# A four-layer graph network on one core: row work of the last group, row buffers, and the end of the program

## The chip, the core and the metric

The kernel runs on one core of a Trainium2 chip. The metric is the device time of one execution in microseconds (us), as the median of several runs. A profile, taken in a separate execution, shows the engines: PE (TensorE) does matrix products into PSUM, DVE (VectorE) and ACT (ScalarE) work elementwise on SBUF and PSUM, POOL (GpSimd) works elementwise on SBUF, SP (SyncE) starts the transfers. PEld is the loading of weights into PE.

## The reference

There are 4096 nodes with 64 features (D = 64) and one adjacency matrix `adj` of 4096 x 4096 zeros and ones in fp32 (64 MB). Four layers follow one another, each as `x = layernorm(x + layer(x, adj))`. Cut to the core:

```python
# layer 0: mean over neighbours, linear, relu, rows to length 1
h = (adj @ X + X) / clip(deg + 1, 1)
out = relu(concat([X, h]) @ W + b);  out / max(norm(out), 1e-12)
# layers 1 and 3: hyperbolic attention (curvature c; c = 1 in layer 3)
adj_att = sigmoid(left[:, None] + right[None, :] + b_att) * adj
x_local = logmap(x[:, None, :], x[None, :, :])
support = einsum('ij,ijd->id', adj_att, x_local)
proj(expmap(x, support))
# layer 2: weight 0.5**(k - pos) for the neighbours in order of index
w = mask * where(pos > 0, 0.5 ** (k - pos), 0.0);  w @ (x @ weight) + bias
```

Since a layer needs every row of the one before, `adj` is read four times.

## The kernel before

`adj` is cut into 4 column stripes of WW = 1024 nodes. The rows of one stripe's nodes are a group; `GROUPS` is (3, 2, 1, 0), so group 0 is the last. A stripe goes over 32 blocks of 128 rows, two at a time (a pair, 1 MB by one transfer from SP's queue into one of six buffers), from block 31 down to 0. So a layer's first stripe needs group 3 at once and group 0 only for the last four pairs (`need((layer, 2 * g // WB))`).

In layers 1 and 3 `attend` does for each block: six matmuls into a PSUM tile z of 128x1024 (L1098 the edges, L1101 and L1104 the products of rows), on ACT the sigmoid of the attention into `sig` (L1113) and the square of z into `sq` (L1116), on DVE `t` = max(z, 0) x sig (L1119, z from PSUM). For each pair DVE then finishes `t` (L1121, 128x2048, `sq` and `t` from SBUF), and PE adds up `acc` from `t` and the row factors `xe` (L1076, eight matmuls), two pairs later. At the end of a stripe ACT copies `acc` to `sums` (L1127).

What happens between two stripes or layers on rows (row work) is written as generators. `move` carries a group's sums to its new rows (centre matmuls L1168, copies L1179, products L1184 and L1185, sums L1187 and L1189, then some 70 steps on 128x8 numbers with three inverse roots, three large steps L1265, L1266, L1269). For the last group it runs on DVE, for the others on GpSimd (`Small(on_pool)`). `end_0` is its counterpart for layer 0 and `end_2` for layer 2; both hand on to `norm_rows` (the layer norm, L896 to L911) and `prepare` (the row factors of the next attention layer, L917 to L1030), whose second half is itself put into a queue. An inverse root is a bit trick for the first value (L724 or L762) and three Newton rounds (L728 to L730 or L767 to L771).

The generators are run by `tick(n)`, called twice in a pair and once more at its end: each turn takes them on to their next `yield`, which gives the turns to wait. Such counts are how long one engine's work is expected to take before another's step is issued. `pool_done(small, large)` is the count for small and large steps on GpSimd; `soon`, `near` and `after` are others. A scheduler orders the instructions of each engine with these positions in view; in layers 0 and 2 PE and ACT keep the written order. An engine executes its instructions in that order, so a step that waits holds up all behind it.

In layer 0 (L1465) the pools m0_own and m0_sb hold `xw`, `sum_w`, `count_w` and the copies `top` and `low` of the accumulators (L1490, L1492). They are given back when the layer ends; the pools of layer 1, with `sig`, take the same space.

Of the kernel before, what the change touches and what calls it, by code (L numbers as in the profile page):

```python
# [19 lines left out]
P = 128  # L20
N = 4096
D = 64
# [29 lines left out]
ROOT2 = 2.0**0.5  # L52
LOG = (0.3333341, 0.1998662, 0.14984541)
# [7 lines left out]
def gnn_stack_kernel(  # L61
# [509 lines left out]
    def stream(fits):  # L571

        with ExitStack() as st:
# [74 lines left out]
            def soon():  # L648


                return 0 if place[0] in (0, 2) else 1
# [16 lines left out]

            spare, turn_of = [], [0]
# [50 lines left out]
            def rsqrt(a, name):  # L720
# [6 lines left out]
                for _ in range(3):  # L727
                    V.tensor_mul(t, r, r)  # L728
                    V.scalar_tensor_tensor(t, t, -0.5, a, ALU.mult, ALU.mult)
                    V.scalar_tensor_tensor(r, t, 1.5, r, ALU.add, ALU.mult)  # L730
                return r

            class Small:
# [19 lines left out]
                def wait(self, small, large=0):  # L753

                    return pool_done(small, large) if self.on_pool else soon()

                def rsqrt(self, a, name, small):

                    r, t = self.nums(name), self.nums("rs_t")
                    if self.on_pool:  # L760
                        yield self.wait(small)
# [4 lines left out]
                    for _ in range(3):  # L766
                        self.mul(t, r, r)  # L767
                        if self.on_pool:
                            self.mul(t, t, a)
                            self.ts(t, t, -0.5, 1.5, ALU.mult, ALU.add)  # L770
                            self.mul(r, t, r)  # L771
                        else:
                            self.stt(t, t, -0.5, a, ALU.mult, ALU.mult)
                            self.stt(r, t, 1.5, r, ALU.add, ALU.mult)
# [41 lines left out]
            def att_rows(w_att, name):  # L816

                t = row.tile([1, 2, 2, D], F32, name=name + "_row")
# [75 lines left out]
            def norm_rows(layer, s, v, x2_to):  # L894
# [12 lines left out]
                r = rsqrt(m, "n_r")  # L907
                yield soon()
                V.tensor_mul(x_of(layer)[:, blocks(s), :], v, over(r))
                V.tensor_mul(x2_to, r, r)  # L910
                V.tensor_mul(x2_to, x2_to, v2)  # L911
                yield soon()

            def prepare(layer, s, att, b_att, curve, least, good, small):
# [5 lines left out]
                V.tensor_scalar(cx2[:, at], x2[:, at], c, None, ALU.mult)  # L920
                V.tensor_scalar(bg, cx2[:, at], -1.0, 1.0, ALU.mult, ALU.add)
# [863 lines left out]
```

## Time and profile before

| what | us |
|---|---|
| median of 3 runs (1074.15 to 1074.6) | 1074.26 |
| the profiled execution's own time | 1069.06 |
| its span on the core | 1067.3 |
| PE busy | 982.1 (92%) |
| DVE busy | 920.2 (86%) |
| ACT busy | 754.3 (71%) |
| POOL busy | 270.8 (25%) |
| DVE L1119, 256 of mean 1.218 | 309.7 |
| DVE L1121, 128 of mean 2.306 | 295.2 |
| PE acc L1076, 1024 matmuls | 260.4 |
| DVE's waits for ACT's squares at L1119 | 14.9 |

Busy times of different engines overlap, so they don't add up to the span; the shares say how full an engine is over the whole. The "sums" copy of ACT (L1127) marks the end of each stripe: 287.05, 364.09, 442.33 and 517.38 in layer 1, and 809.77, 886.49, 962.96 and 1038.34 in layer 3. The layer-0 stripes end with L1490 at 53.64, 95.67, 139.26 and 181.06, the layer-2 accumulators are copied (L1685) at 610.20, 661.15 and 716.66.

### The profile page before, as it was taken

How to read it: one execution, taken by the hardware profiler on the slowest of the kernel's cores; microseconds unless marked ns; L12 is line 12 of the kernel's file. 1: busy time of each engine (PE TensorE's matmuls, PEld its weight loads, DVE VectorE, ACT ScalarE, POOL GpSimd, SP SyncE). 2: the span in 40 equal slices, each digit the busy share in tenths (PEclk: the TensorE clock that was granted, in tenths of full speed). 3: DMA queues.
4: the chain of work that ended last, by engine and by line, in shares of the span. 5: the costliest groups of instructions: out<-in, count | busy, mean ns of one | idle time of the engine just before them, and what ended most of it. 6: DMA issues, size and time to landing. Idle time of an engine off the chain costs nothing.

```text
span 1067.3 us, 13569 instructions
## 1 busy us (share of the span) xinstructions
PE 982.1 (92%) x4760; PEld 403.2 (38%) x4845; DVE 920.2 (86%) x1501; ACT 754.3 (71%) x877; POOL 270.8 (25%) x649
## 2 busy tenths in 40 slices
PE   5997998789999999999999999998899999999980
PEld 2454554333333333333333344443333333333320
DVE  8577887899999999999485489849999999999976
ACT  0013122779988899888677788898898888898850
POOL 0011212010044515435500010101102454444163
PEclk8899999989999999999999999999999999999985
DMA  9999999745656656757598999996465766666300
GB/s 364 356 426 364 383 395 375 277 175 197 233 204 230 215 206 202 249 184 249 205 363 332 371 346 316 324 321 222 138 236 190 250 216 208 241 228 234 131 1 24
DMA packets 38580, 271.62 MB, mean 254 GB/s; under 512 B 4710, under 2 KB 4710, under 8 KB 5734
## 3 DMA queue, kind: packets, MB, share of 16 engines
q1 hardware_dynamic: 37728, 270.03, 69.3%
q8 instruction: 40, 0.66, 0.2%
q10 hardware_dynamic: 774, 0.63, 0.2%
q14 instruction: 38, 0.31, 0.1%
HBM read 269.58 MB, written 1.05 MB: 254 GB/s over the span
## 4 chain that ended last, share of the span: by engine, by line
PE 66%; DVE 22%; ACT 5%; DMA 2%; POOL 2%; issue 2%; ACTq 0%; SPq 0%; POOLq 0%
PE acc L1076 17%; PE z L1641 11%; PE z L1101 8%; PE z L1098 7%; PE z L1104 7%; DVE t L1119 7%; DVE t L1121 6%; PE acc L1465 6%; PE z L1653 3%; DVE junk L844 2%; PE z L1607 2%; DMA edges<-in_adj_dram 2%; ACT sq L1648 1%; ACT sq L1116 1%; POOL sq L1435 1%
## 5 line engine op out<-in xcount | busy, mean ns | idle before, releaser
L1119 DVE SCALAR_TENSOR_TENSOR t<-z,sig 128x1024 f32<-128x1024 f32 x256 | 309.7, 1218 | 16.9 <-ACT sq L1116 14.9
L1121 DVE SCALAR_TENSOR_TENSOR t<-sq,t 128x2048 f32<-128x2048 f32 x128 | 295.2, 2306 | 0.2
L1116 ACT ACTIVATE sq<-z 128x1024 f32<-128x1024 f32 x256 | 254.3, 1021 | 56.5 <-PE z L1104 21.6
L1113 ACT ACTIVATE sig<-left_b,right 128x1024 f32<-128x1024 f32 x256 | 286.9, 1149 | 5.3 <-DVE t L1119 4.5
L1076 PE MATMUL acc<-t,xe 128*64 128x512 f32 x1024 | 260.4, 614 | 10.9 <-DVE t L1121 9.3
L1101 PE MATMUL z<-lo_hi,hi_lo 128*128 128x512 f16 x512 | 193.7, 378 | 3.8 <-issue 0.9
L1104 PE MATMUL z<-dst,src 74*128 74x512 f16 x512 | 194.7, 380 | 0.0
L1098 PE MATMUL z<-edges,two_i 128*128 128x512 bf16 x463 | 181.7, 392 | 5.4 <-DVE t L1119 5.4
L1648 ACT ACTIVATE sq<-z 128x512 bf16<-128x512 f32 (+1 forms) x192 | 137.6, 740 | 40.1 <-PE z L1641 39.5
L1076 PEld LDWEIGHTS acc<-t,xe 128*64 128x64 f32 x1024 | 64.3, 137 | 140.6 <-issue 106.5
L1098 PEld LDWEIGHTS <-two_i 128*128 128x128 bf16 x512 | 50.2, 98 | 120.7 <-issue 74.5
L1465 PE MATMUL acc<-edges,first 128*128 128x512 bf16 x241 | 77.9, 400 | 16.5 <-DMA edges<-in_adj_dram 15.9
L1641 PE MATMUL z<-edges,pass_by 128*128 128x512 bf16 x240 | 84.7, 388 | 7.3 <-ACT sq L1648 6.0
L844 DVE SCALAR_TENSOR_TENSOR t<-edges 128x2048 bf16<-128x2048 f32 x32 | 73.0, 2287 | 19.6 <-DMA edges<-in_adj_dram 19.2
L1641 PE MATMUL z<-edges,enter 128*128 128x512 bf16 x251 | 86.8, 387 | 0.5
L844 DVE SCALAR_TENSOR_TENSOR junk<-edges 128x2048 bf16<-128x2048 f32 x32 | 73.1, 2284 | 13.1 <-DMA edges<-in_adj_dram 13.1
L1465 PE MATMUL acc<-edges,third 128*65 128x512 bf16 x256 | 80.9, 397 | 0.8 <-issue 0.2
L1104 PEld LDWEIGHTS <-src 74*128 74x128 f16 x512 | 49.1, 96 | 72.0 <-issue 9.2
L1101 PEld LDWEIGHTS <-hi_lo 128*128 128x128 f16 x512 | 50.2, 98 | 60.6 <-issue 14.5
L901 POOL TENSOR_TENSOR sq<-z 128x512 f32<-128x512 f32 x8 | 10.2, 1278 | 156.1 <-DVE z L900 144.8
L1184 POOL TENSOR_TENSOR w_att<-x,u 128x512 f32<-128x512 f32 x6 | 12.7, 2121 | 140.9 <-ACT u L1179 140.9
L1607 PE MATMUL z<-sq,halves 128*128 128x512 bf16 x120 | 45.1, 377 | 0.7 <-ACT sq L1648 0.5
(399 smaller groups left out, 965.0 us busy)
## 6 DMA issues: line engine op xcount, KB each, us to landing
edges<-in_adj_dram SPq DMA_DIRECT2D x256, 1024.0 KB, 4.9
x<-in_x_dram SPq DMA_DIRECT2D x4, 256.0 KB
out_dram<-x ACTq DMA_DIRECT2D x2, 256.0 KB
out_dram<-x SPq DMA_DIRECT2D x2, 256.0 KB
w_sb<-in_L_gnn_W_dram ACTq DMA_DIRECT2D x1, 32.0 KB, 4.8
w_twice<-in_L_gnn_weight_dram ACTq DMA_DIRECT2D x2, 16.0 KB, 4.8
given<-in_L_gnn_b_dram ACTq DMA_DIRECT2D x1, 0.2 KB
given<-in_L_gnn_bias_dram ACTq DMA_DIRECT2D x1, 0.2 KB
```

What stands on the lines that cost most here:

```text
L844: V.scalar_tensor_tensor(junk, a, 0.0, a, ALU.not_equal, ALU.not_equal, accum_out=odd[:, n : n + 1])
L1076: it = nc.tensor.matmul(acc[h * D : (h + 1) * D, :], xe[:, j, :], t[:, k, h * W : (h + 1) * W], start=j == BLOCKS[0], stop=j == BLOCKS[-1],)
L1098: nc.tensor.matmul(half, two_i, edge[:, at : at + W], start=True, stop=False)
L1101: nc.tensor.matmul(half, hi_lo[:, of], lo_hi[:, to], start=False, stop=False)
L1104: last = nc.tensor.matmul(half, src[:, of], dst[:, to], start=False, stop=True)
L1113: nc.scalar.activation(sig, left_b, AF.Sigmoid, bias=right[:, j : j + 1])
L1116: nc.scalar.activation(sq[:, k], zp, AF.Square, bias=ROOT + OFF, scale=-1.0 / UNIT)
L1119: V.scalar_tensor_tensor(t[:, k], zp, 0.0, sig, ALU.max, ALU.mult)
L1121: V.scalar_tensor_tensor(t, sq, HIGH**2, t, ALU.add, ALU.mult)
L1465: nc.tensor.matmul(accs[h][:m], lhs[:, j, :], edge[:, at : at + W], start=j == BLOCKS[0], stop=j == BLOCKS[-1],)
L1641: nc.tensor.matmul(z[:, h : h + W], lhs, rhs[:, h : h + W], start=j == BLOCKS[0], stop=True, skip_group_check=True,)
L1648: weighed[0] = nc.scalar.activation(w, z[:, :n], AF.Exp, bias=-(OFF_EDGE + CUT) * LN2, scale=-LN2)
```

## The change

It has five parts.

- In the first stripes of layers 1 and 3 the last group's rows are still in preparation. Its large (128x512) steps and inverse roots move from DVE to GpSimd, all but the roots' first value and the sums along rows; so do small steps between them. `far` gives the wait counts.
- The inverse root has one round of higher order and one Newton round in place of three Newton rounds: seven steps on DVE instead of nine after the first value, ten on GpSimd instead of twelve.
- Row buffers: `xw` lies in `halves`, `sum_w` and `count_w` in `keep`, `top` and `low` and the attention rows in row tiles, and the pool m0_sb goes.
- The wait counts for GpSimd are shorter outside layer 2 (`Small.wait`), and two `soon` turns in `move` are left out for it.
- At the end of the program the last pair's `t` is two tiles, each finished by a 128x1024 step and added up by itself. The last `move` (`straight`) puts both parts' centre matmuls into two z tiles; the square, the product and the last product with q read PSUM directly, and ACT copies only the column of sums. Besides, the copy of layer 2's last accumulator is on DVE instead of ACT.

The diff, cut to its core and with the common indentation of eight places left out (the repeated signature of `add_up`, the call of `att_rows` and the dropped pool are not shown):

```diff
@@ -50,6 +50,7 @@
+THIRD = 0.375**0.5
@@ -666,6 +667,11 @@
+    def far(small, large=0):
+        beat = {1: 0.8, 3: 0.4}.get(place[0], 1.6)
+        return 1 + int((small * 0.29 + large * 1.04 + 2.3) / beat)
@@ -724,10 +730,13 @@
         )
-        for _ in range(3):
-            V.tensor_mul(t, r, r)
-            V.scalar_tensor_tensor(t, t, -0.5, a, ALU.mult, ALU.mult)
-            V.scalar_tensor_tensor(r, t, 1.5, r, ALU.add, ALU.mult)
+        V.tensor_mul(t, r, r)
+        V.scalar_tensor_tensor(t, t, THIRD, a, ALU.mult, ALU.mult)
+        V.scalar_tensor_tensor(t, t, -10.0 / 3.0 * THIRD, t, ALU.add, ALU.mult)
+        V.scalar_tensor_tensor(r, t, 5.0 * THIRD**2, r, ALU.add, ALU.mult)
+        V.tensor_mul(t, r, r)
+        V.scalar_tensor_tensor(t, t, -0.5, a, ALU.mult, ALU.mult)
+        V.scalar_tensor_tensor(r, t, 1.5, r, ALU.add, ALU.mult)
         return r
@@ -752,26 +761,40 @@
-            return pool_done(small, large) if self.on_pool else soon()
+            if not self.on_pool:
+                return soon()
+            if place[0] == 2:
+                return pool_done(small, large)
+            return 1 + int((small * 0.29 + large * 1.04 + 2.3) / 1.6)
...
-            if self.on_pool:
+            if self.on_pool and small:
...
-            for _ in range(3):
+            self.mul(t, r, r)
+            if self.on_pool:
+                s = self.nums("rs_s")
+                self.mul(t, t, a)
+                self.ts(s, t, 0.375, -1.25, ALU.mult, ALU.add)
+                self.mul(t, t, s)
+                self.ts(t, t, 1.875, None, ALU.add)
+                self.mul(r, t, r)
...
-                if self.on_pool:
-                    self.mul(t, t, a)
-                    self.ts(t, t, -0.5, 1.5, ALU.mult, ALU.add)
-                    self.mul(r, t, r)
-                else:
-                    self.stt(t, t, -0.5, a, ALU.mult, ALU.mult)
-                    self.stt(r, t, 1.5, r, ALU.add, ALU.mult)
+                self.mul(t, t, a)
+                self.ts(t, t, -0.5, 1.5, ALU.mult, ALU.add)
+                self.mul(r, t, r)
+            else:
+                self.stt(t, t, THIRD, a, ALU.mult, ALU.mult)
+                self.stt(t, t, -10.0 / 3.0 * THIRD, t, ALU.add, ALU.mult)
+                self.stt(r, t, 5.0 * THIRD**2, r, ALU.add, ALU.mult)
+                self.mul(t, r, r)
+                self.stt(t, t, -0.5, a, ALU.mult, ALU.mult)
+                self.stt(r, t, 1.5, r, ALU.add, ALU.mult)
@@ -813,9 +836,13 @@
-    def att_rows(w_att, name):
...
-        t = row.tile([1, 2, 2, D], F32, name=name + "_row")
+    att_space = grp("xw")[:1].rearrange("o k f -> o (k f)")
...
+    def att_rows(w_att, n):
...
+        t = att_space[:, n * 4 * D : (n + 1) * 4 * D].rearrange(
+            "o (u k d) -> o u k d", u=2, k=2
+        )
@@ -896,20 +923,29 @@
+        pooled = s == GROUPS[-1]
+        E = nc.gpsimd if pooled else V
...
-        V.tensor_sub(v, v, over(m))
+        E.tensor_sub(v, v, over(m))
...
-        yield soon()
-        yield soon()
+        if pooled:
+            yield far(0, 2)
+        else:
+            yield soon()
+            yield soon()
...
-        r = rsqrt(m, "n_r")
-        yield soon()
-        V.tensor_mul(x_of(layer)[:, blocks(s), :], v, over(r))
-        V.tensor_mul(x2_to, r, r)
-        V.tensor_mul(x2_to, x2_to, v2)
-        yield soon()
+        if pooled:
+            r = yield from Small(True, "").rsqrt(m, "n_r", 0)
+        else:
+            r = rsqrt(m, "n_r")
+            yield soon()
+        E.tensor_mul(x2_to, r, r)
+        E.tensor_mul(x2_to, x2_to, v2)
+        E.tensor_mul(x_of(layer)[:, blocks(s), :], v, over(r))
+        if not pooled:
+            yield soon()
@@ -917,15 +953,19 @@
-        V.tensor_scalar(cx2[:, at], x2[:, at], c, None, ALU.mult)
-        V.tensor_scalar(bg, cx2[:, at], -1.0, 1.0, ALU.mult, ALU.add)
+        pooled = s == GROUPS[-1]
+        E = nc.gpsimd if pooled else V
+        E.tensor_scalar(cx2[:, at], x2[:, at], c, None, ALU.mult)
+        E.tensor_scalar(bg, cx2[:, at], -1.0, 1.0, ALU.mult, ALU.add)
+        if pooled:
+            yield far(14, 1)
...
-        V.tensor_scalar(rbg, rbg, -0.13, 0.0, ALU.max, ALU.min)
+        E.tensor_scalar(rbg, rbg, -0.13, 0.0, ALU.max, ALU.min)
...
-        V.tensor_scalar(ym, rbg, sc, None, ALU.mult)
-        V.tensor_mul(y, xg, over(ym))
+        E.tensor_scalar(ym, rbg, sc, None, ALU.mult)
+        E.tensor_mul(y, xg, over(ym))
@@ -944,27 +984,32 @@
-            V.tensor_sub(ys[:, :, D : 2 * D], y, ys[:, :, :D])
+            E.tensor_sub(ys[:, :, D : 2 * D], y, ys[:, :, :D])
...
-            yield 1
-            V.tensor_add(w, xg, over(g))
-            yield 1
-            V.tensor_mul(xe[:, at, :], w, over(m))
+            if not pooled:
+                yield 1
+            E.tensor_add(w, xg, over(g))
+            if not pooled:
+                yield 1
+            E.tensor_mul(xe[:, at, :], w, over(m))
...
-            rt = rsqrt(q1, "rt")
-            V.tensor_mul(t, q1, rt)
-            V.tensor_scalar(t, t, TOP, None, ALU.min)
-            V.tensor_scalar(q1, q1, QTOP, None, ALU.min)
+            if pooled:
+                rt = yield from Small(True, "").rsqrt(q1, "rt", 0)
+            else:
+                rt = rsqrt(q1, "rt")
+            E.tensor_mul(t, q1, rt)
+            E.tensor_scalar(t, t, TOP, None, ALU.min)
+            E.tensor_scalar(q1, q1, QTOP, None, ALU.min)
...
-            yield 2 * near()
+            yield far(10, 1) if pooled else 2 * near()
@@ -1028,7 +1073,7 @@
-        later(second(), True, after(small))
+        later(second(), True, far(2, 1) if pooled else after(small))
         yield 1
@@ -1109,6 +1154,9 @@
                     t = sb.tile([P, 2, WW], F32, name="t", bufs=3)
+                    ts = [t, t]
+                    if g == 0 and then is None and layer == 3:
+                        ts[0] = sb.tile([P, 2, WW], F32, name="t", bufs=3)
                 sig = sb.tile([P, WW], F32, name="sig", bufs=3)
@@ -1116,10 +1164,17 @@
-                V.scalar_tensor_tensor(t[:, k], zp, 0.0, sig, ALU.max, ALU.mult)
+                V.scalar_tensor_tensor(ts[k][:, k], zp, 0.0, sig, ALU.max, ALU.mult)
...
-            V.scalar_tensor_tensor(t, sq, HIGH**2, t, ALU.add, ALU.mult)
-            lag.append((g, t))
+            if ts[0] is t:
+                V.scalar_tensor_tensor(t, sq, HIGH**2, t, ALU.add, ALU.mult)
+                lag.append((g, t, (1, 0)))
+            else:
+                for k in (1, 0):
+                    V.scalar_tensor_tensor(
+                        ts[k][:, k], sq[:, k], HIGH**2, ts[k][:, k], ALU.add, ALU.mult
+                    )
+                    lag.append((g, ts[k], (k,)))
@@ -1160,7 +1215,37 @@
-        for part in range(2):
+        straight = last and layer == 3
+        parts = []
+        if straight:
...
+            def part_of(rows, part):
+                of = slice(2 * part, 2 * part + 2)
+                return rows.rearrange("p (h k) f -> p k h f", h=2)[:, of]
...
+            for part in range(2):
+                t = z_tile()[:, : 4 * (D + 1)].rearrange(
+                    "p (i h f) -> p i h f", i=2, h=2
+                )
+                for i in range(2):
+                    cols = slice((2 * part + i) * P, (2 * part + i + 1) * P)
+                    nc.tensor.matmul(
+                        t[:, i], sums[:, cols], centre, start=True, stop=True
+                    )
+                parts.append(t)
+            yield near()
+            for part, t in enumerate(parts):
+                nc.scalar.activation(part_of(sq, part), t[:, :, :, :D], AF.Square)
+                V.tensor_mul(part_of(w, part), part_of(xg, part), t[:, :, :, :D])
+            for part, t in enumerate(parts):
+                nc.scalar.copy(
+                    sum_1.rearrange("p (h k) -> p k h", h=2)[
+                        :, 2 * part : 2 * part + 2
+                    ],
+                    t[:, :, :, D],
+                )
+            yield near()
+        for part in () if straight else range(2):
@@ -1181,14 +1266,16 @@
-        E.tensor_mul(w, xg, u)
-        nc.scalar.activation(sq, u, AF.Square)
-        yield G.wait(0, 1) if G.on_pool else near()
+        if not straight:
+            E.tensor_mul(w, xg, u)
+            nc.scalar.activation(sq, u, AF.Square)
+            yield G.wait(0, 1) if G.on_pool else near()
...
-        yield soon()
-        yield soon()
+        if not G.on_pool:
+            yield soon()
+            yield soon()
@@ -1263,7 +1350,11 @@
         E.tensor_mul(w, xg, over(p))
-        E.tensor_mul(u, u, over(q))
+        if straight:
+            for part, t in enumerate(parts):
+                V.tensor_mul(part_of(u, part), t[:, :, :, :D], part_of(over(q), part))
+        else:
+            E.tensor_mul(u, u, over(q))
         yield soon()
@@ -1362,9 +1452,9 @@
-        xw = own.tile([P, NB, D], F32, name="xw")
-        sum_w = own.tile([P, D + 1], F32, name="sum_w")
-        count_w = own.tile([D + 1, D + 1], F32, name="count_w")
+        xw = halves.bitcast(F32)
+        sum_w = keep.tile([P, D + 1], F32, name="sum_w")
+        count_w = keep.tile([D + 1, D + 1], F32, name="count_w")
@@ -1436,11 +1526,17 @@
-            n = rsqrt(n2, "n")
-            yield 1
-            V.tensor_mul(z, z, over(n))
-            V.tensor_add(z, z, x0[:, blocks(s), :])
-            yield 1
+            if s == GROUPS[-1]:
+                n = yield from Small(True, "").rsqrt(n2, "n", 0)
+                nc.gpsimd.tensor_mul(z, z, over(n))
+                nc.gpsimd.tensor_add(z, z, x0[:, blocks(s), :])
+                yield far(10, 2)
+            else:
+                n = rsqrt(n2, "n")
+                yield 1
+                V.tensor_mul(z, z, over(n))
+                V.tensor_add(z, z, x0[:, blocks(s), :])
+                yield 1
@@ -1486,9 +1582,15 @@
-                    top = sb.tile([P, W], F32, name="top")
+                    top = row.tile([P, W], F32, name="sums", bufs=2)
...
-                    low = sb.tile([D + 1, W], F32, name="low")
+                    low = (
+                        row.tile([P, WB, D + 1], F32, name="u_1").rearrange(
+                            "p k f -> p (k f)"
+                        )[: D + 1, :W]
+                        if h
+                        else grp("w_att").rearrange("p k f -> p (k f)")[: D + 1]
+                    )
@@ -1682,7 +1784,10 @@
                 for to, acc in zip(sums, of):
-                    nc.scalar.copy(to, acc)
+                    if s == GROUPS[-1]:
+                        V.tensor_copy(to, acc)
+                    else:
+                        nc.scalar.copy(to, acc)
                 later(end_2(s, sums))
```

More of the change, by code (lines that the diff above doesn't have):

```diff
@@ L1069, in attend, with add_up @@
                 lag = []
-                def add_up(g, t, behind=None):
-                    for k in (1, 0):
+                def add_up(g, t, ks, behind=None):
+                    for k in ks:
                         j = 2 * g + k
@@ L1355, in stream @@
                 own = lp.enter_context(tc.tile_pool(name="m0_own", bufs=1))
-                sb = lp.enter_context(tc.tile_pool(name="m0_sb", bufs=2))
                 ps = lp.enter_context(tc.tile_pool(name="m0_ps", bufs=6, space=PSUM))
@@ L1401, in stream @@
                 nc.scalar.dma_start(sum_w[:D, :D], w0[D:, :])
-                att_rows1, att_rows3 = att_rows(w_att1, "att1"), att_rows(w_att3, "att3")
+                att_rows1, att_rows3 = att_rows(w_att1, 0), att_rows(w_att3, 1)
                 def own_part(at, t):
```

## The prediction

> **What bounds the kernel now.** I read the page's busy shares and its chain first: PE is busy 92% of the 1067.3 us span and holds 66% of the chain, DVE 86% and 22%. Such shares mix four layers, so I cut the span with the windows view (columns: window, its length, busy PE, PEld, DVE, ACT, POOL with instruction counts, granted clock, DMA share, GB/s):
>
> ```profile
> 200.00:225.00 25.00, 22.29 (x94) 7.46 (x96) 25.00 (x41) 21.54 (x23) 1.04 (x1) 1.00 0.58 199
> 225.00:250.00 25.00, 21.80 (x104) 8.87 (x105) 21.29 (x53) 19.07 (x22) 4.69 (x7) 0.86 0.33 114
> 250.00:275.00 25.00, 24.86 (x111) 9.16 (x112) 24.07 (x23) 24.31 (x26) 0.00 (x0) 1.00 0.71 250
> ...
> 750.00:775.00 25.00, 21.58 (x113) 8.67 (x114) 22.96 (x59) 20.17 (x24) 4.67 (x7) 0.93 0.40 143
> ...
> 950.00:975.00 25.00, 24.86 (x107) 8.53 (x109) 24.37 (x20) 21.94 (x24) 11.21 (x36) 1.00 0.65 221
> ...
> 1025.00:1050.00 25.00, 12.63 (x42) 4.27 (x39) 16.75 (x33) 4.96 (x8) 16.60 (x55) 0.65 0.01 2
> 1050.00:1068.00 18.00, 0.00 (x0) 0.00 (x0) 10.72 (x64) 0.21 (x1) 0.30 (x1) 0.50 0.09 33
> ```
>
> Three regimes. In a settled stripe of layers 1 and 3 PE is full (24.86 of 25): a pair costs it 4.62 us, DVE 2 x 1.13 + 2.20 = 4.47. Nothing taken from DVE there shortens it. In the first stripe of those layers DVE is full and PE idles: DVE also prepares the last group's rows. From the starts of the `sums` copy, L1127 (287.05, 364.09, 442.33, 517.38; 809.77, 886.49, 962.96, 1038.34) a settled stripe takes 75 to 78 us; the first one takes 102 in layer 1 (first z matmul 185.02) and 95.7 in layer 3 (714.08). That is the room: at most some 25 and 19 us, much of it PE's own start. The third regime is the end, 1032 to 1067, a chain of small steps. Layers 0 and 2 are held by transfers (0.93 of the engines in 175 to 200) and by PE. Their edits I cost at nothing: shorter roots there lie beside these, and the layer-0 copies into rows that now alternate wait for reads of a stripe earlier, 42 us back (L1490 at 53.64, 95.67, 139.26). Were that cover gone, it would be a root's 1.9 us per stripe.
>
> One more thing the trace shows: GpSimd and DVE delay each other (timelines; columns start, length, engine, operation).
>
> ```profile
> 1015.09 2.28 DVE L1121 SCALAR_TENSOR_TENSOR t<-sq,t 128x2048 f32<-128x2048 f32 x1
> ...
> 1015.20 2.23 POOL L767 TENSOR_TENSOR rs_t<-r_t 128x8 f32<-128x8 f32 x1
> ```
>
> That GpSimd step usually takes 0.20. It lasts as long as the L1121 begun just before it. The other way round, at the end of the program:
>
> ```profile
> 1046.96 0.17 DVE L747 SCALAR_TENSOR_TENSOR r_t<-rs_t,r_t 128x8 f32<-128x8 f32 x1
> 1047.16 0.90 DVE L767 TENSOR_TENSOR rs_t<-r_t 128x8 f32<-128x8 f32 x1
> 1048.09 0.96 DVE L747 SCALAR_TENSOR_TENSOR rs_t<-rs_t,t 128x8 f32<-128x8 f32 x1
> ...
> 1049.29 1.03 DVE L767 TENSOR_TENSOR rs_t<-r_t 128x8 f32<-128x8 f32 x1
> ```
>
> ```profile
> 1046.97 1.06 POOL L1265 TENSOR_TENSOR w_att<-x,p 128x512 f32<-128x512 f32 x1
> 1047.99 1.04 POOL L1266 TENSOR_TENSOR u<-u,q 128x512 f32<-128x512 f32 x1
> 1049.11 1.19 POOL L1269 TENSOR_TENSOR x<-u,w_att 128x512 f32<-128x512 f32 x1
> ```
>
> Three DVE steps of 0.17 wait out the three large GpSimd steps.
>
> **Layer 1's first stripe: buffers, GpSimd, shorter roots.** Removed from DVE: eight 128x512 steps (L1441, L1442, L900, L909, L928, L947, L953, L955), 0.60 each between L1119s = 4.8; three roots of ten steps, of which only the seed stays, and some dozen small steps: at 0.075 to 0.2 each, some 4.1 net. Together 8.9. The start also moves. In before, ACT's first sigmoid waits until DVE has read the buffers that `sig` lies over:
>
> ```profile
> ACT L1113 <- DVE z L1429: 5.3, 1, 5.3
> ```
>
> and the first L1119 stands behind L1433, the reduction and a root of 1.9 us: it starts at 193.66. With the rows moved, `sig` waits for nothing and L1119 stands before L1433 in DVE's order: about 189.2. The first L1121 comes at 192.5 instead of 197.85, a lead of 5.3.
>
> Added: waits of DVE for GpSimd, and whatever DVE holds behind a waiting step stands too, L1119 and L1121 above all, so PSUM tiles stay full and PE stops. I replayed the new order by hand with the rule that one of the two waits out the other: the mean (waits for two 128x512 steps of 1.04 that collide with an L1121) 1.8; the variance sum 1.1; the reciprocal 2.6; L1121s behind GpSimd's y and xe steps 1.6 and 0.9: 8.0 in all. So DVE gains 5.3 + 8.9 - 8.0 = 6, between 5 and 8 as I vary the phase. PE can't use all of it: with its busy windows and its slower clock (0.86 in one) put end to end, without any wait for DVE, the copy at 287.05 could come at 272 at best, and spread over pairs I get a lead of 4.6. I take **-4.5**; bounds -11 (half of the stalls gone, near PE's end) and -1 (5.3 alone, with stalls a half above mine). The faster stripe asks for transfers sooner; their share of 0.33 to 0.71 here leaves room.
>
> Here a rule speaks against the change. The Trainium skill, "Perfetto Trace Analysis", section Optimizing Scalar/DVE Operations, says of moves between GpSimd and DVE that, since they share a port, they might not help; "SBUF — State Buffer", section Who interferes with whom, narrows it: a DVE instruction with at most one SBUF input doesn't contend. L1119 reads z from PSUM and only `sig` from SBUF; L1121 reads two from SBUF. By the first rule the 4.8 us of large steps come back in full (8 x 1.04 us of GpSimd blocking), leaving 5.3 + 4.1 - 8.0, so about -1.4. By the rows, which show a block only beside L1121 (half of DVE's time), it is the sum above. I follow the rows.
>
> **Layer 3's first stripe.** The start gains 1.0: the copy of layer 2's last accumulator (two L1685 rows, 716.66 to 717.71, in ACT's row, which is busy 23.54 of 25 there) goes to DVE, which idles there from 714.6 to 718.67. Six 128x512 steps: 3.6; roots and small steps 2.3; two DVE waits for GpSimd of before (0.93 and 2.04) go: 3.0. Against it waits of 1.0 (variance), 3.65 (reciprocal, behind a whole L1121 on GpSimd's side), 0.8 and 2.4 (the logarithm on ACT now wants GpSimd's root): 7.9. PE has a bound here of about 802 against 809.8. DVE's sum says -2, the stalls lie late in the stripe where no slack follows; I take **-1**, between +3 and -7.5.
>
> **Settled stripes.** GpSimd's part of `move` has shorter wait counts: of the four waits 5 to 4, 6 to 4, 5 to 4, 8 to 6 turns, and two turns dropped, eight in all at 4.62 / 3 = 1.54 us each: it ends some 12 us sooner. PE binds here, so this earns nothing by itself; if DVE reaches its next step before GpSimd is done, it stalls with L1119 behind it. The free GpSimd time between L1121s is about 3.4, 10.2, 3.4 and 5.7 us for needs of 2.6, 7.3, 2.7 and 4.9: all fit. **+0.3**, at most +3.
>
> **The end.** Five terms:
> - the last 128x2048 step becomes two of 1.1, so four of the last eight accumulations start earlier. They run at 0.46 each now (PE row at 1034.61: 3.68 for eight). By the row alone the last step gives about -1.0. "TensorE: Matmul & The Clock Gate", section Part 1, wants some 3.4 us of sustained work for the full rate, so closing PE's pause of 1.0 before them might give the full 0.23: -2.8. The pause only halves and the clock is 0.65 in this window: -1.2;
> - both centre matmul pairs go back to back (1.24 each, ACT copies between them at present), squares and products from PSUM: `d` ends at 1043.05 instead of 1044.78: -1.75;
> - the root at 1046.55 to 1050.73 takes 4.18; nine clean steps are 1.83, and GpSimd is done sooner, so its three blocks vanish: -2.35;
> - three roots on DVE have two steps less, 6 x 0.20: -1.2;
> - the last u times q from PSUM in two halves: +0.1.
>
> Sum **-6.4**, between -5 and -8. The output transfer behind it (1062.43 to 1067.3) stays.
>
> **Sum.** -4.5 - 1 + 0.3 - 6.4 = -11.6 on the profiled execution, 1069.06, so 1057.5. The median of the runs shown is 1074.26, 0.5% above it; the same step gives **1062.7**.
>
> **Rivals.**
> - *Only the end pays* (0.21). The windows speak for it: in 200 to 225 DVE is full, and every us taken from it may return as a wait for GpSimd. Against it: the 5.3 us start is no exchange between engines. First stripes 0: -6.1, 1068.2.
> - *Waits cost more than the steps* (0.10), the other side. Each time that GpSimd starts just after an L1121, as at 1015.20, it loses 2.2 us, and DVE's dependent step then stands in front of the next L1121. I have 15.9 us of such waits in both first stripes; doubled they take 16 more: -11.6 + 16 = +4.4, 1078.7. The turning point is 27.5 us in total.
> - *PE binds throughout* (0.12): the waits halve, 8 us come back: -19.6, 1054.7. For it: seeds and waits stand several slots apart. Against it: PE's own start and clock cap what it can use.
> - *The change doesn't do what it says* (0.02): against it, in the new order the steps do stand in GpSimd's row, and DVE has 125 instructions less, GpSimd 46 more. That leaves 1074.
> - Forecast case 0.55.
>
> **How the numbers follow.** The forecast case spans 1058 to 1067: layer 1 and layer 3 vary by some 3 each, the end by 1.5. A measurement here tells 0.2%, 2.1 us, from no change. Of the slow case most is above that (0.07); same takes the rest, the unchanged case and the upper tail of "only the end" (0.05); faster 0.88. Range 1055.5 to 1071.
>
> **What would show it.** First L1119 of layer 1 near 189 and no 5.3 wait on ACT; the `sums` copies of layer 1 4 to 5 us sooner, the first of layer 3 another 1; DVE waits for GpSimd below 16 us in the two stripes; at the end `d` 1.7 us sooner after the copy, the root in 1.4 us, last copy to end of span in 23.7 instead of 29.0. It is wrong if DVE's row shows GpSimd waits above 20 us in a first stripe, if the settled stripes grow beyond 78 us, or if the last GpSimd move still runs beside the root.

## The result, and the profile after

The changed kernel takes 1068.19 us in the median of 7 runs (1063.63 to 1070.72), the kernel before 1074.06 (7 runs, 1070.35 to 1074.6): ratio 0.9952, interval 0.993 to 0.9974. By this ratio that is 5.1 us (the two medians differ by 5.9), where 11.6 were forecast. A second series of 22 runs gave 0.9954 (0.9935 to 0.9973). The windows of the profiled execution of the changed kernel, same columns and stretches as before:

```profile
200.00:225.00 25.00, 18.81 (x81) 6.32 (x79) 19.65 (x21) 17.32 (x18) 17.71 (x26) 1.00 0.64 220
225.00:250.00 25.00, 20.86 (x106) 8.18 (x104) 19.20 (x37) 19.32 (x23) 11.54 (x24) 0.86 0.29 90
250.00:275.00 25.00, 24.78 (x113) 9.16 (x112) 23.94 (x17) 24.59 (x26) 0.00 (x0) 1.00 0.70 247
...
750.00:775.00 25.00, 23.59 (x125) 9.28 (x123) 21.32 (x33) 23.36 (x26) 5.79 (x9) 1.00 0.56 194
...
950.00:975.00 25.00, 25.00 (x111) 8.99 (x107) 22.84 (x16) 22.05 (x25) 11.82 (x12) 1.00 0.64 221
...
1025.00:1050.00 25.00, 14.14 (x58) 4.76 (x56) 20.99 (x57) 7.87 (x12) 9.45 (x16) 0.84 0.04 14
1050.00:1068.00 18.00, 0.00 (x0) 0.00 (x0) 6.95 (x38) 0.00 (x0) 0.00 (x0) 0.58 0.05 17
```

From 200 to 225 DVE went from 25.00 to 19.65 busy, GpSimd from 1.04 to 17.71. But PE, which the relief was meant for, went down too, from 22.29 to 18.81. DVE was relieved and nobody used it.

The fastest and the slowest execution of one kernel lie 4 to 13 us apart, so I compare stages, taken from the starts of the copies. "Layer 1 start" runs from the last layer-0 copy to the end of the first eight sums of products; "rest" from there to the first `sums` copy; "layer 3 first" from the copy of layer 2's last accumulator to the `sums` copy; "last + end" is the last stripe and what follows, to the end of the span. All in us, from one profile each:

| kernel | layer 1 start | rest | layer 3 first | last + end |
|---|---|---|---|---|
| before | 20.1 | 84.9 | 93.1 | 104.3 |
| changed | 15.0 | 88.8 | 96.6 | 97.4 |
| changed, again (after_again) | 15.0 | 88.4 | 96.7 | 95.8 |
| no_gp | 15.0 | 85.2 | 92.3 | 96.7 |
| no_gp1 | 19.2 | 86.8 | 96.7 | 95.9 |
| no_gp3 | 15.0 | 88.5 | 93.3 | 96.1 |
| before_rows | 15.0 | 89.1 | 94.3 | 104.4 |
| no_gp_old_roots | 15.0 | 92.3 | 92.8 | 96.1 |
| ys_first | 15.0 | 86.7 | 96.8 | 96.4 |
| long_waits | 15.0 | 86.6 | 99.2 | 97.2 |
| mixed | 19.2 | 86.6 | 93.5 | 96.6 |
| rb_late3 | 18.1 | 88.2 | 92.3 | 96.8 |
| before_end | 20.6 | 84.8 | 93.0 | 103.8 |
| no_gp_old_counts | 18.1 | 85.2 | 93.4 | 102.5 |

So the end brought 7 to 8.6 us, layer 1's first stripe 1.3 to 1.6, and layer 3's took back 3.5. (The copy that opens it, now on DVE, starts 1.7 us sooner after the copy of the accumulator before it, so the net loss around it is 1.8.) The settled stripes of layer 1 are each within some 0.5 us of before (0.2 in sum); in layer 3 the second and third together are 1.0 longer in the changed kernel's profile and 2.0 in its repeat, most of it in the third (76.5 before, 77.2 and 78.2).

Where it goes in layer 1: DVE's steps that wait for GpSimd (timeline; the wait in front of a step and who ended it stand at the end of the row), and the two PE rows behind them:

```profile
205.18 0.69 DVE L924 TENSOR_REDUCE n_m<-z 128x8 f32<-128x512 f32 x1 [2.14 <-POOL z L1532]
...
211.35 0.69 DVE L936 TENSOR_REDUCE n_v<-sq 128x8 f32<-128x512 f32 x1 [0.93 <-POOL sq L930]
...
223.47 0.20 DVE L962 RECIPROCAL rb<-b 128x8 f32<-128x8 f32 x1 [2.23 <-POOL b L959]
```

```profile
230.44 1.03 PE L1023 MATMUL aux<-ident,ys 128*128 128x128 f16 x8 [4.14 <-POOL ys L987]
231.40 3.68 PE L1121 MATMUL acc<-t,xe 128*64 128x512 f32 x8
```

These three DVE waits are about those of the forecast (1.8, 1.1, 2.6). The 4.14 us is not in it: PE's transposes of the last group's `ys` stand in its queue ahead of sums and z that were ready, and `ys` now comes from GpSimd. After this pause eight sums take 3.68 instead of 1.94, which I call half rate, and DVE in turn stands 4.02 us for ACT's next square. In layer 3 the same happens through DVE (DVE timeline, then PE's):

```profile
737.57 0.20 DVE L962 RECIPROCAL rb<-b 128x8 f32<-128x8 f32 x1 [3.70 <-POOL b L959]
737.69 2.24 DVE L1170 SCALAR_TENSOR_TENSOR t<-sq,t 128x2048 f32<-128x2048 f32 x1
```

```profile
739.98 3.68 PE L1121 MATMUL acc<-t,xe 128*64 128x512 f32 x8 [3.82 <-DVE t L1170]
```

A step of 0.20 us waits 3.70; L1170 behind it waits too; PE has nothing to sum for 3.82 and then runs at half rate for another 3.68. One handoff costs PE 3.82 + 1.74 = 5.6 us. In the kernel before, DVE's only wait for GpSimd of over 0.4 us in this stripe is one of 0.93, and PE's longest pause is 1.48.

### The profile page after: what moved, and what is told of

Its sections match the earlier page's. It is cut to its first block, busy times and chain, and to the rows that moved or that the text cites. A ratio compares the mean times of both kernels' runs of the same rounds, so it can differ in the third digit from the quotient of the medians.

```text
span 1063.3 us, 13594 instructions
## 1 busy us (share of the span) xinstructions
PE 985.4 (93%) x4845; PEld 400.7 (38%) x4845; DVE 901.2 (85%) x1383; ACT 753.4 (71%) x876; POOL 339.1 (32%) x695
## 4 chain that ended last, share of the span: by engine, by line
PE 66%; DVE 18%; POOL 5%; DMA 4%; ACT 4%; issue 2%; ACTq 0%; SPq 0%; POOLq 0%; DVEq 0%
PE acc L1121 18%; PE z L1743 11%; PE z L1143 8%; PE z L1149 8%; PE z L1146 7%; DVE t L1170 5%; DVE t L1167 5%; PE acc L1561 4%; DMA edges<-in_adj_dram 3%; PE z L1755 3%; DVE junk L871 2%; PE z L1709 2%; ACT sq L1750 1%; ACT sq L1164 1%; POOL sq L1525 1%
## 5 line engine op out<-in xcount | busy, mean ns | idle before, releaser
L1170 DVE SCALAR_TENSOR_TENSOR t<-sq,t 128x2048 f32<-128x2048 f32 x127 | 293.4, 2311 | 0.3
L1143 PE MATMUL z<-edges,two_i 128*128 128x512 bf16 x512 | 200.3, 391 | 6.2 <-DVE t L1167 6.2
L1561 PE MATMUL acc<-edges,first 128*128 128x512 bf16 x256 | 81.1, 398 | 18.1 <-DMA edges<-in_adj_dram 17.9
L1743 PE MATMUL z<-edges,enter 128*128 128x512 bf16 x256 | 88.2, 387 | 0.0
L1270 POOL TENSOR_TENSOR w_att<-x,u 128x512 f32<-128x512 f32 x6 | 18.2, 3028 | 169.9 <-ACT u L1264 169.9
L1709 PE MATMUL z<-sq,halves 128*128 128x512 bf16 x128 | 48.1, 377 | 0.6 <-ACT sq L1750 0.6
L1525 POOL TENSOR_TENSOR sq<-z 128x512 f32<-128x512 f32 x4 | 10.1, 2526 | 117.2 <-DVE z L1523 97.4
```

The lines of the kernel that those rows point to most:

```text
L1143: nc.tensor.matmul(half, two_i, edge[:, at : at + W], start=True, stop=False)
L1170: V.scalar_tensor_tensor(t, sq, HIGH**2, t, ALU.add, ALU.mult)
L1561: nc.tensor.matmul(accs[h][:m], lhs[:, j, :], edge[:, at : at + W], start=j == BLOCKS[0], stop=j == BLOCKS[-1],)
L1743: nc.tensor.matmul(z[:, h : h + W], lhs, rhs[:, h : h + W], start=j == BLOCKS[0], stop=True, skip_group_check=True,)
```

## Experiments: which part costs, which pays

All are made from the changed kernel unless said otherwise, and every row of the table above is one of their profiles.

**GpSimd's share taken back, in both layers or in one.**

```diff
-                pooled = s == GROUPS[-1]
+                pooled = False                           # no_gp
+                pooled = s == GROUPS[-1] and layer == 3  # no_gp1
+                pooled = s == GROUPS[-1] and layer == 1  # no_gp3
```

(and likewise for the root n of layer 0's end in no_gp and no_gp1.)

> The changed kernel once more, as the yardstick for the three beside it. Both theories: 0.993 to 0.998 of the kernel before; layer 1's first stripe (last layer-0 copy to first sums copy) 104 to 106 us against 105 before, layer 3's first stripe (copy of layer 2's last accumulator to sums copy) 96 to 97 against 93 before, last sums copy to end of span 23 to 24 against 29.

> The changed kernel with the last group's roots and large steps back on VectorE in both layers; row buffers, shorter roots, shorter counts and the new end are kept. Theory A (waits between VectorE and GpSimd stop TensorE, and its slow clock after a pause adds to it): layer 1's first stripe 100 to 102, layer 3's 92 to 93, so 5 to 7 us below the changed kernel, ratio to before 0.987 to 0.990. Theory B (the moved steps do pay, and the missing gain went elsewhere, such as transfers): 4 us or more above the changed kernel, ratio to before 0.998 or more. Theory C (TensorE and transfers set the first stripes anyway): within 1 us of the changed kernel.

> The steps back on VectorE in layer 1 alone. Theory A: layer 1's first stripe 100 to 102 as without any moved step, layer 3's 96 to 97 as in the changed kernel; 2.5 to 4 us below the changed kernel. Theory B: layer 1's first stripe 107 or more. Theory C: both stripes as in the changed kernel within 1 us.

> The steps back on VectorE in layer 3 alone. Theory A: layer 3's first stripe 92 to 93.5, layer 1's as in the changed kernel; 3 to 4.5 us below the changed kernel. Theory B: layer 3's first stripe above 97. Theory C: both stripes as in the changed kernel within 1 us.

Measured ratios to before: no_gp 0.9892 (0.9858 to 0.9926), no_gp1 0.9916 (0.9884 to 0.9949), no_gp3 0.9911 (0.9878 to 0.9944), beside 0.9954 for the changed kernel. Theory A holds, B and C fall: with both starts undisturbed, the steps moved to GpSimd cost 3.2 to 3.6 us in layer 1's rest (no_gp against the changed kernel), and 3.4 to 4.4 in layer 3. Without them the change is worth 1.1%, the size of the forecast. The repeat of the changed kernel missed one expectation: its first stripe took 103.4, not 104 to 106.

no_gp1's whole first stripe (105.97) missed its 100 to 102, and its rest (86.8) is 1.6 above no_gp's, though its program for layer 1 is no_gp's. The windows of no_gp and of no_gp1, in this order, show what befell the start:

```profile
185.00:195.00 10.00, 9.82 (x70) 5.65 (x70) 6.62 (x9) 8.59 (x10) 1.04 (x1) 1.00 1.01 425
```

```profile
185.00:195.00 10.00, 9.17 (x51) 6.88 (x50) 1.90 (x6) 7.11 (x9) 0.00 (x0) 0.70 1.01 420
```

PE's granted clock was 0.70 there in this execution, and its start took 19.2 instead of 15.0. (Layer 0 ends 3.5 us later in no_gp1, but no_gp is at 1.00 throughout 180 to 205.) This befell four of the profiles (18.1 to 19.2 in the table), so start and rest are kept apart. Whether the slow start also explains the 1.6 of the rest stays open: no_gp_old_counts has such a start too, and a rest of 85.2.

**Only the row buffers, on the kernel before.** The edit: `xw`, `sum_w`, `count_w`, `top`, `low` and the attention rows moved as in the change, nothing else.

> The kernel before with only the row buffers moved. Theory A: the whole lead at the start of layer 1 is this part: ACT's 5.3 us wait goes, the first sum of products ends 15 us after the last layer-0 copy as in the changed kernel (20.1 before), and it lasts: layer 1's first stripe 99.5 to 101, ratio 0.994 to 0.997. Rival: VectorE is full behind it and the lead is lost by the end of the stripe: 103.5 to 105, ratio 0.999 or more. Everything from layer 1's second stripe on as before within 0.5 us a stripe.

Ratio 0.9988 (0.9969 to 1.0008): no difference that can be told. The lead is there (15.0 instead of 20.1) and is gone at the end (89.1 instead of 84.9): the rival was right. DVE's row in before_rows shows where:

```profile
264.45 2.36 DVE L1123 SCALAR_TENSOR_TENSOR t<-z,sig 128x1024 f32<-128x1024 f32 x2 [4.29 <-ACT sig L1117]
```

This is the thirteenth pair. Its `sig` needs the last group's `right`, which is finished 76.7 us after the last layer-0 copy, as late as ever (74.5 before). The pairs came earlier and waited for the rows. The expectation of everything else within 0.5 us a stripe missed: the second stripe is 1.3 shorter, layer 3's first 1.2 longer, the last stripe 1.8 shorter and what follows it 1.8 longer. So an edit can move other stages by 1 to 2 us. What a stage varies without any edit, the two profiles of the changed kernel show: 0.4 us in the rest, 0.1 in layer 3's first stripe, 1.6 in the last one and the end.

**The shorter roots taken back**, from no_gp: three rounds again in DVE's `rsqrt`.

> The kernel no_gp (no step of the last group on GpSimd) with VectorE's inverse roots of three rounds again. Theory D2 (the pairs that need the last group wait for its preparation, and a root costs this chain a slot between two large steps for each of its steps; the moved rows only pay if the chain is shorter too): layer 1's first stripe 103 to 105 as in before_rows (104.1; 100.2 in no_gp), with a wait of 3 to 5 us of VectorE for ACT's sig ahead of the thirteenth pair; layer 3's 93.5 to 95. Theory E (shorter roots only save their own VectorE time, some 1.5 us): 100.5 to 101.7 and 92.3 to 93.3, no such wait. Both: last sums copy to end of span 1.2 us longer than no_gp's 23.1.

Ratio 0.9953 (0.9933 to 0.9974). Layer 1's stripe is 107.3, its rest 7.1 us longer than no_gp's, more than either theory said, and the wait is there:

```profile
266.57 3.49 DVE L1164 SCALAR_TENSOR_TENSOR t<-z,sig 128x1024 f32<-128x1024 f32 x3 [5.89 <-ACT sig L1158]
```

D2 holds in layer 1, E falls. Most of a root's dependent steps stand between two large steps of DVE, as no_gp's row shows:

```profile
219.74 0.16 DVE L733 TENSOR_TENSOR rs_t<-n_r 128x8 f32<-128x8 f32 x1
219.82 1.22 DVE L1167 SCALAR_TENSOR_TENSOR t<-z,sig 128x1024 f32<-128x1024 f32 x1
220.95 0.16 DVE L734 SCALAR_TENSOR_TENSOR rs_t<-rs_t,n_m 128x8 f32<-128x8 f32 x1
```

I call such a place a slot: two steps less are up to two slots less. With shorter roots in no_gp, `right` is finished at 72.7 instead of 77.1, and pair thirteen no longer waits. These 4.4 us are not the whole 7.1: behind the missed date PE pauses too and then runs at half rate for some 6 us (z matmuls of 0.63 instead of 0.38, PE's row in no_gp_old_roots), worth about 3 us by an estimate from these rows.

```profile
267.85 0.59 PE L1140 MATMUL z<-edges,two_i 128*128 128x512 bf16 x1 [3.01 <-DVE t L1164]
268.23 0.63 PE L1143 MATMUL z<-lo_hi,hi_lo 128*128 128x512 f16 x1
```

Layer 3 (92.8, forecast 93.5 to 95 by D2) lies with E: no deadline was missed there. The end missed both: at 23.0 after the copy it did not lengthen, since this edit leaves alone the second root function, which the end uses.

**ys first on GpSimd.**

```diff
-                    E.tensor_sub(ys[:, :, D : 2 * D], y, ys[:, :, :D])   # behind copies and xw
+                    ys_low = E.tensor_sub(ys[:, :, D : 2 * D], y, ys[:, :, :D])
+                    for it in its: in_order(it.ins, ys_low.ins)          # copies, xw
```

> The changed kernel with one thing moved: for the last group GpSimd subtracts ys (which TensorE's transposes wait for) ahead of the small copies and of xw, instead of behind them. Theory A1 (TensorE standing 4.1 us for GpSimd's ys, and half clock after it, is the larger part of what layer 1 loses): the wait falls below 2 us and layer 1's first stripe to 100.3 to 101.7, from 103.4 to 103.8. Theory A2 (the waits of VectorE for GpSimd decide, TensorE's pause only takes time that VectorE could not have used): layer 1's first stripe within 0.8 us of the changed kernel. Both: layer 3's first stripe stays at 96 to 97, since TensorE didn't wait for ys there.

The rest falls from 88.4 to 88.8 to 86.7, the stripe to 101.6: A1's upper edge. But the wait is still 2.59, because `ys` itself meets an L1170 and lasts 2.54 instead of 1.1 (GpSimd's row, then PE's):

```profile
223.46 2.54 POOL L972 TENSOR_TENSOR ys<-y,ys 128x512 f16<-128x512 f32 x1 [0.73 <-ACT ys L971]
```

```profile
226.06 1.03 PE L1026 MATMUL aux<-ident,ys 128*128 128x128 f16 x8 [2.59 <-POOL ys L972]
227.03 3.68 PE L1124 MATMUL acc<-t,xe 128*64 128x512 f32 x8
```

So this order takes back about 2 us of the 3.2 to 3.6, by one profile. What is left isn't divided: the shorter pause with its half rate and DVE's waits, unchanged here (2.14, 0.93, 2.23), both stand. Ratio 0.9946 (0.9924 to 0.9967), not told from the changed kernel by time alone.

**All of the preparation's wait counts doubled**, `beat = {1: 0.4, 3: 0.2}.get(place[0], 0.8)`.

> The changed kernel with the wait counts of the last group's preparation doubled, so that VectorE meets the sums, the reciprocal and the next steps one to three pairs later. Theory A2 (VectorE comes too early and stands with the pairs behind it): its waits for GpSimd (n_m 2.1, n_v 0.9, rb 2.2 in layer 1; n_v 1.2, rb 3.7 in layer 3) fall below 1 us in each stripe, layer 3's first stripe to 93 to 94.5 from 96.6, layer 1's to 100 to 102. Theory D (the longer chain on GpSimd itself is the cost, and only changes the place of the wait): both stripes as long as in the changed kernel within 0.8 us, or longer, with the wait at the transposes or at the pairs that need group 0.

Ratio 0.9953 (0.9932 to 0.9974). Half of each theory: DVE's waits for GpSimd are gone in layer 1 (the twelfth L1170 starts 65.6 us after the last layer-0 copy, 79.0 in the changed kernel), but the rows come late (`right` at 73.6 instead of 66.0) and the thirteenth starts only at 80.1. The stripe, 101.5, lies in A2's range all the same. In layer 3 the stripe grows to 99.2, as D said. There PE stands at the transposes, by now behind ACT:

```profile
769.10 1.01 PE L1023 MATMUL aux<-ident,ys 128*128 128x128 f16 x8 [4.95 <-ACT hi_lo L1027]
770.04 3.67 PE L1121 MATMUL acc<-t,xe 128*64 128x512 f32 x8
```

**One wait alone, one pair later, in layer 3.**

```diff
-                    yield far(14, 1)
+                    yield far(14, 1, 1.6 if layer == 3 else 1.0)   # last: factor on the count
```

> The changed kernel with one count longer: in layer 3 VectorE meets the last group's reciprocal one pair later (two L1119 steps and one L1121 step more in front of it). If VectorE's 3.7 us wait there, TensorE's pause of 3.8 us and the half clock after it are what layer 3 loses: the wait falls below 0.5 us, the 3.68 us for eight sums returns to 1.94, and layer 3's first stripe is 92.5 to 94.5 (96.65 in the changed kernel, 93.1 before). If the later end of the preparation takes it back: 96 or more, with waits at the transposes. Layer 1 as in the changed kernel; ratio to before 0.990 to 0.994.

DVE's order differs by one pair in front of one reciprocal. DVE's and PE's rows answer to the two of the changed kernel above:

```profile
742.33 0.20 DVE L962 RECIPROCAL rb<-b 128x8 f32<-128x8 f32 x1 [1.09 <-POOL b L959]
```

```profile
744.75 1.94 PE L1121 MATMUL acc<-t,xe 128*64 128x512 f32 x8 [1.18 <-DVE t L1170]
```

The wait is 1.09 (not below 0.5), PE's pause 1.18, the sums are back at 1.94, and layer 3's first stripe is 92.3: 4.3 us less. That is all that layer 3 had lost (no_gp has 92.3 too), with every other step still on GpSimd. Ratio 0.9878 (0.9818 to 0.9938, 4 runs), better than expected, though too wide an interval to tell from 0.990.

**A mixed version**: GpSimd in layer 1 only, `ys` first, longer counts ahead of the mean, the variance and the reciprocal, the last root on DVE.

> GpSimd helps in layer 1 only, ys is subtracted first, the wait counts ahead of the mean, the variance and the reciprocal are longer, and the last root (rt) is back on VectorE. If waits that come too early and a chain that ends too late are the two costs: VectorE's and TensorE's waits for GpSimd below 1.5 us in all, no wait for sig above 2 us, layer 1's first stripe 95 to 99 (no_gp 100.2, changed kernel 103.5), layer 3's 92 to 93.5; ratio to before 0.984 to 0.990. If the chain on GpSimd is too slow in any placing: layer 1's first stripe 101 or more.

Ratio 0.9865 (0.9839 to 0.989), 4 runs: faster than before and than the changed kernel, and not told from no_gp. Its first stripe took 105.7 instead of 95 to 99; without some 4 us of slow start (19.2) that is 101.5, within the other case's "101 or more". So this run doesn't show that GpSimd's chain could pay in layer 1 in any placing. Its counts may have been too long: `right` is finished at 81.3 (with the slow start in it), PE waits 2.96 for `ys` and 4.21 around the thirteenth pair, DVE 2.06 for `sig`, and the rest is 86.6 against no_gp's 85.2.

**The new end alone, on the kernel before** (two tiles and `straight`, old roots and counts).

> The kernel before with only the end of the program changed (two tiles, straight). By the prediction's sum: last stripe 1.2 us shorter (75.4 to 74.2; 72.6 if the slow clock of the last sums goes altogether), last sums copy to end of span 1.7 us shorter (28.96 to 27.3), because the inverse root still stands beside GpSimd's three large steps. If those 2.35 us do not come from that meeting but from the steps' own places: 25 or less. Ratio 0.996 to 0.998.

Ratio 1.0002 (0.9984 to 1.0019): nothing. After the copy it takes 30.2 instead of 27.3. DVE's row:

```profile
1041.40 0.68 DVE L1228 TENSOR_REDUCE uu<-xw 128x8 f32<-128x512 f32 x1
1045.27 0.17 DVE L762 TENSOR_SCALAR n<-w 128x8 int32<-128x8 int32 x1 [3.19 <-POOL w L1301]
1045.35 0.68 DVE L1230 TENSOR_REDUCE d<-y 128x8 f32<-128x512 f32 x1
```

The straight path is ready early, and DVE then stands 3.19 us at the first value of a root of the group before last, for which GpSimd's `w` is not ready; `d` is behind it. The kernel before has this wait too, longer, and the prediction did not read it:

```profile
1042.64 0.17 DVE L762 TENSOR_SCALAR n<-w 128x8 int32<-128x8 int32 x1 [5.49 <-POOL w L1260]
```

There it hid behind ACT's copies, which ended at about the same time. Its date hangs on GpSimd's move and not on the end: 79.5 to 80.0 us after the third `sums` copy in all four kernels with the old counts (before, before_rows, before_end, no_gp_old_counts), and 58.6 to 59.1 in the changed kernel.

**Old wait counts, from no_gp** (`pool_done` for all places, and the two `soon` turns).

> The kernel no_gp with the old wait counts for GpSimd. If the gain at the end hangs on the counts (GpSimd's last move must be over before VectorE's end begins): last stripe and what follows together 101 to 104 us, against 96.7 in no_gp and 104.3 in the kernel before, with VectorE waiting 2 us or more for GpSimd's L1247 or L1260 work in front of the reduction to d. If the new end pays by itself: 97 to 98.5. Settled stripes in both cases within 0.5 us of no_gp.

Last stripe and end 102.5, in the range of the first case; the old counts take back 5.9 of 7.7 us. DVE's row, again:

```profile
1034.45 0.73 DVE L1239 TENSOR_TENSOR y<-x,z 128x256 f32<-128x256 f32 x2
1039.19 0.17 DVE L775 TENSOR_SCALAR n<-w 128x8 int32<-128x8 int32 x1 [4.02 <-POOL w L1346]
1039.27 0.68 DVE L1273 TENSOR_REDUCE uu<-xw 128x8 f32<-128x512 f32 x1
```

Ratio 0.9912 (0.9886 to 0.9939), 4 runs. The settled stripes missed their forecast: with the old counts layer 3's third takes 75.9 us, 78.2 in no_gp, so the shorter counts cost some 2 us there.

## Why the prediction was wrong

**The failed step** is the sum for layer 1, "So DVE gains 5.3 + 8.9 - 8.0 = 6", and the one made like it for layer 3, "DVE's sum says -2 ... I take -1". They set DVE's busy time that was removed against DVE's waits, as if a full DVE were what bounds the first stripe; its own windows had DVE full from 200 to 225, but at 21.29 of 25 in the stretch after it. Term by term, the forecast was -4.5, -1, +0.3 and -6.4; measured were -1.3 to -1.6 in layer 1's first stripe, +1.8 around layer 3's, about +1 to +2 in the settled ones and -7.0 to -8.6 at the end.

- The lead of 5.3 came: 5.1 in every kernel with the buffers moved, undisturbed starts compared. But before_rows shows that it is worth about 1 us of stripe by itself: pairs that come early wait for the last group's rows. It pays with the shorter roots (no_gp).
- The 8.9 us of DVE time was worth nothing as time. What a step on DVE costs here is its place in a chain with a date, the thirteenth pair. Root steps were booked at 0.075 to 0.2 us each; two fewer in each of three roots are worth 7.1 us of rest in layer 1, with PE's half rate after the missed date in it. GpSimd shortens this chain further (`right` at 66.0 instead of no_gp's 72.7), but the pairs, held up at the handoffs, come later than the rows: the twelfth L1170 starts at 79.0 instead of 73.9.
- The 8.0 and 7.9 of waits were, if anything, too large: DVE waited 2.14 + 0.93 + 2.23 = 5.3 us for GpSimd in layer 1 and 1.22 + 3.70 = 4.9 in layer 3 (there 1.30 more for ACT's logarithm, where 2.4 was booked), far from the 20 us named as a sign of being wrong. What was left out is what they do to PE: the transposes that wait for GpSimd's `ys` (4.14), and the half rate after such a pause (1.74 each time). How layer 1's 3.2 to 3.6 divides between the waits of PE and of DVE is open: ys_first, which shortens PE's wait alone, and long_waits, where these waits for GpSimd are gone but the rows come late, each take back about 2.
- Layer 3's sum had a misread term besides: of the two waits for GpSimd that were to go (0.93 and 2.04), the second stands in DVE's row as one for PE (`lr<-aux`, L991), and the first came back as 1.22. "The stalls lie late in the stripe where no slack follows" was the right thought at the wrong size: with the start's gain in it, as in the -1, +1.8 was measured.
- The rule of "Perfetto Trace Analysis", section Optimizing Scalar/DVE Operations, that moves between GpSimd and DVE might not help described the outcome, though its reason here isn't the shared port alone. GpSimd's small steps beside L1170 do stretch (2.17 to 2.28 us instead of 0.20), as the rows had said; what made it dear in layer 3 is a DVE that works in order and meets the result too soon (rb_late3).

**The end** was right in total (-6.4; measured -7.0 and -8.6) and mixed in its terms. `d` ends 3.87 us after the copy instead of 6.44, more than the 1.75 put down for the straight path; in the kernel before, its product also stood behind the step that waits for GpSimd, but what each is worth there isn't separated. The root is clean (DVE's row of the changed kernel):

```profile
1043.24 0.68 DVE L1275 TENSOR_REDUCE d<-y 128x8 f32<-128x512 f32 x1
...
1045.71 0.17 DVE L779 TENSOR_TENSOR rs_t<-r_t 128x8 f32<-128x8 f32 x1
...
1046.91 0.17 DVE L756 SCALAR_TENSOR_TENSOR r_t<-rs_t,r_t 128x8 f32<-128x8 f32 x1
```

1.37 us against 4.18: the 2.35 and 0.4 as forecast. That the terms hang together was missed: the two tiles and the straight path alone are worth 0.6 in these stages (before_end), and the shorter counts, which I had put among the settled stripes at +0.3, are what frees them; there they cost 1 to 2 us, inside the +3 allowed. That the total fits is in part luck: the last stripe's share of it (1.3 and 2.6) comes without the two tiles as well (next section but one).

**The rivals.** "Only the end pays" (1068.2) is what happened to the time, by a way of its own: layer 1 gave a little and layer 3 took it. The reason for it, that what is taken from DVE returns as a wait, is half of the cause; the date of the chain is the other half and stood in no case. That the time lies in the stated range, 1055.5 to 1071, it owes to the end alone.

## What to carry to other kernels

When row work is fed between the steps of a full pipeline, count the chain's slots against the date at which its result is needed, not the busy time that it takes: two steps less in each of three roots were worth 7 us, eight large steps moved away less than nothing (3.2 to 3.6 us lost). A move to another engine is as good as its worst handoff: look in the order of each engine at what stands behind the first step that uses the result, and put that step later before judging the move. Parts of a change can need each other: the row buffers alone gave 0.1%, the new end alone nothing, and together with the roots and the counts, without GpSimd's share, they gave 1.1%.

## What the runs showed of the hardware

PE's rate after a pause isn't settled by the length of the pause. Pauses of 3.82 and 4.14 us were followed by half rate, as "TensorE: Matmul & The Clock Gate", section Part 1, would have it, which sets the half rate after an idle window of some 3.4 us. But so were pauses of 2.59 (ys_first) and 3.01 (no_gp_old_roots), and the last eight sums ran at full rate after 1.52 us in before_rows, yet at half rate after 1.01 in the kernel before. PE's rows in the kernel before, in before_rows and in the changed kernel's repeat:

```profile
1034.61 3.68 PE L1076 MATMUL acc<-t,xe 128*64 128x512 f32 x8 [1.01 <-DVE g L1718]
```

```profile
1034.90 1.94 PE L1080 MATMUL acc<-t,xe 128*64 128x512 f32 x8 [1.52 <-DVE g L1727]
```

```profile
1036.16 1.94 PE L1121 MATMUL acc<-t,xe 128*64 128x512 f32 x8 [2.13 <-DVE t L1170]
1038.42 2.22 PE L1121 MATMUL acc<-t,xe 128*64 128x512 f32 x8 [0.33 <-DVE t L1174]
```

In the changed kernel's first profile the same sixteen took 5.35 in one row, after a pause of 2.23. So the 1.2 us of the two tiles can't be told from this: the last stripe is 75.4, 73.6 and 73.6 with the kernels before, before_rows and before_end, and 74.1 and 72.8 with the changed one. The clock's dip at layer 1's start in four profiles is as little explained: PE pauses 0.82 us there in no_gp and goes on at full rate, and 0.83 in no_gp1 and goes on at half. It lengthens that start by 3 to 4 us, of the size of the scatter between runs.
